# Reading the moving operand of the energy matmuls backwards in a self-attention kernel

## The chip, the cores and the metric

The kernel runs on one core of a Trainium2 chip. The metric is the device time of one execution in microseconds (us). TensorE is called PE in the profile, and its weight loads, which run beside its matmuls, are shown as an engine of their own, PEld. VectorE is DVE, ScalarE is ACT, GpSimd is POOL, SyncE is SP.

## The reference

The input x has the shape (4, 64, 64, 256): four images b, each with N = 4096 positions. Per image:

- q = x Wq + bq and k = x Wk + bk, 128 channels each; v = x Wv + bv, 256 channels.
- q, k and v are taken as matrices with N columns by reshaping the flat array, not by transposing it (`q.reshape(B, -1, N)`).
- energy[n, m] = sum over c of q[c, n] k[c, m]; attention = softmax over m; out[c, n] = sum over m of v[c, m] attention[n, m].
- The result is gamma * out + x, all in float32.

A query n is a column of q; whatever order the columns are worked on in, each has its own softmax and its own output column.

## The kernel before, in words

**Tiles and loops.** Per image b there are 16 groups g of 256 queries (NB = 256, NJ = 2 halves j of 128), and per group 8 steps t of 4 blocks of 128 keys each, 128 steps u = 8 g + t per image and 512 in all. Every float32 product is made of three float32r products: each operand is split into a high half h, a remainder l and a combined form d (`halved`, lines 260 to 269; `halves`, 352 to 361).

**One step on TensorE** is 36 matmuls, each with a weight load of its own (128 columns):

- *Energies* (`energy`, lines 317 to 339): 12 matmuls at line 330. The weights are a 128x128 block of k in form f (tile `k`), the moving operand is the whole form f of q, 256 columns (tile `q`). Two of three go to the PSUM tile `sa`, the third to `sb`. They are made three steps ahead (LOOK = 3): while step u is attended, the energies of u + 3 are made. ScalarE takes the exponential (line 334), VectorE multiplies the two parts (344), ScalarE and VectorE make h, l and d of the result (349, 355, 358).
- *Attend* (`attend`, lines 363 to 391): 24 matmuls at line 380, in the order h, l, d; within each, half j = 0 and then 1; within each half, four key blocks i = 0 to 3. The weights are 128 columns of h, l or d, the moving operand is a row of `vh`, `vl` (258 columns, two of ones for the softmax sums) or `vd` (256 columns). The row is m = 2t + i // 2 + 16 (i % 2). The h and l products of half j are added up in the PSUM tile `a`*j* over the whole group, the d products in `bb`. So the last four products of l (j = 1) stand directly before the eight of d.

Rows of `vh` and `vl` lie 260 elements apart, those of `vd` 256; the tiles of q and k have rows of 256 and 128 elements.

**Order of the work.** The order is written out by hand (`manual_schedule`). In each step of the main loop (lines 507 to 549): the energies of u + 3 in two halves k = 0, 1, `join` and `upper` after the first, then the weights of a later step are fetched by `load_k` on POOL's queue, then `halves`, then `attend`, with pieces of the finish of the previous group between (`proceed`). While a group is finished (`finish`, lines 400 to 422), VectorE scales the sums, TensorE transposes the 256 queries back (line 417, tile `ot`, once in a group), VectorE adds the input `xr` to it (line 421) and POOL's queue writes the result out (422). The very last group has its own form, `finish_last` (lines 440 to 466), with two adds at line 465 and the last write on SP's queue. Between two images, 16 rounds of projections (lines 116 to 173) run through TensorE, with the first energies beside them.

Three tiles named `pad` (lines 208 to 212) hold nothing and shift the addresses of the pools after them.

Of the kernel before, what the change touches and what calls it, by code (L numbers as in the profile page):

```python
# [13 lines left out]
ALU = mybir.AluOpType  # L14
# [6 lines left out]
def kernel(  # L21
# [36 lines left out]
    nc = tc.nc  # L58
    B, W, H, C = x.shape
    P = 128  # L60
# [115 lines left out]
    NJ = NB // P  # L176
# [24 lines left out]
    with ExitStack() as fast:  # L201
# [115 lines left out]
        def energy(b, u, k):  # L317

            g, t = divmod(u, NU)
            if k == 0:  # L320
                x = ppool.tile([P, 4, NB], F32, tag="x", name=f"x_{b}_{u}", bufs=3)
                y = ppool.tile([P, 4, NB], F32, tag="y", name=f"y_{b}_{u}")
                units[b, u] = x, y
            x, y = units[b, u]
            q, kt = loads[b, "q", g], loads[b, "k", u]
            sa = ps_s.tile([P, 2, NJ, P], F32, tag="a", name=f"sa_{b}_{u}_{k}")
            sb = ps_s.tile([P, 2, NJ, P], F32, tag="b", name=f"sb_{b}_{u}_{k}")
            for i in range(2):
                for to, f, first, last in ((sa, 0, True, False), (sa, 1, False, True), (sb, 2, True, True)):
                    nc.tensor.matmul(  # L330
                        to[:, i], kt[:, 2 * k + i, f, :], q[:, f], start=first, stop=last
                    )
            for to, sp, scale in ((x, sa, (1.0 + E) / E), (y, sb, -1.0 / E)):
                nc.scalar.activation(  # L334
                    to[:, 2 * k : 2 * k + 2, :],
                    sp.rearrange("p i j d -> p i (j d)"),
                    AF.Exp,
                    scale=scale,
                )
# [23 lines left out]
        def attend(b, u):  # L363

            g, t = divmod(u, NU)
            if t == 0:
                now["acc"] = [
                    ps_o.tile([P, C + 2], F32, tag=f"a{j}", name=f"a{j}_{b}_{g}")
                    for j in range(NJ)
                ]  # L370
                now["bb"] = ps_o.tile([P, NJ, C], F32, tag="bb", name=f"bb_{b}_{g}")
            h, l, d = units[b, u]
            acc, bb = now["acc"], now["bb"]
            for left, right in ((h, vh), (l, vl), (d, vd)):
                for j in range(NJ):
                    out_ = bb[:, j, :] if left is d else acc[j]
                    for i in range(4):
                        m = 2 * t + i // 2 + NI * (i % 2)

                        nc.tensor.matmul(  # L380
                            out_,
                            left[:, i, j * P : (j + 1) * P],
                            right[:, m, : out_.shape[1]],
                            start=(t == i == 0 and (left is h or left is d and j == 0)),
                            stop=(t == NU - 1 and i == 3 and left is not h),
                            skip_group_check=True,
                        )
            if t == NU - 1 and (b, g) != (B - 1, NG - 1):
                o = now["o"] = work.tile([P, NJ, C + 2], F32, tag="o", name=f"o_{b}_{g}")
                for j in range(NJ):  # L390
                    nc.scalar.activation(o[:, j, :], acc[j], AF.Identity, scale=1.0 + E)

        def factors(b, g, gamma):

            r = work.tile([P, 2, NJ], F32, tag="r", name=f"r_{b}_{g}")
            nc.vector.reciprocal(r[:, 0, :], zall[:, b * NG + g, :])
            nc.vector.tensor_tensor(r[:, 0, :], r[:, 0, :], gamma.to_broadcast([P, NJ]), ALU.mult)
            return r[:, 0, :], r[:, 1, :]

        def finish(b, g, o, bb, xr):  # L400
            yield
            yield

            nc.vector.tensor_copy(zall[:, b * NG + g, :], o[:, :, C])
            r, _ = factors(b, g, gam1)
            nc.vector.tensor_tensor(o[:, :, :C], o[:, :, :C], bb, ALU.add)
            yield
            for j in range(NJ):
                nc.scalar.activation(
                    o[:, j, :C], o[:, j, :C], AF.Identity, scale=r[:, j : j + 1]  # L410
                )
            yield
            yield
            tp = ps_t.tile([P, 2, NB], F32, tag="t", name=f"ot_{b}_{g}")
            for s in range(2):
                for j in range(NJ):
                    nc.tensor.transpose(
                        tp[:, s, j * P : (j + 1) * P], o[:, j, s * P : (s + 1) * P], ident
                    )
            yield  # L420
            nc.vector.tensor_tensor(xr, xr, tp, ALU.add)
            nc.gpsimd.dma_start(ov[b, g], xr)

        def guard():

            z = zall.rearrange("p n j -> p (n j)")
            ok = ppool.tile([P, 4, NB], F32, tag="y", name="ok")[:, 0, : B * NG * NJ]
            nc.vector.tensor_scalar(ok, z, Z_LOW, None, ALU.is_ge)
            nc.vector.scalar_tensor_tensor(ok, z, Z_HIGH, ok, ALU.is_le, ALU.mult)
            yield  # L430
            nc.vector.tensor_reduce(zs, ok, AX.X, ALU.min)
            nc.vector.tensor_scalar(zs, zs, 0.5, None, ALU.is_lt)
            zp = ps_s.tile([P, 1], F32, tag="b", name="zp")
            nc.tensor.matmul(zp, ones, zs, start=True, stop=True)
            yield
            nc.vector.tensor_copy(again, zp)
            yield
            yield

        def finish_last(b, g, xr):  # L440

            for j in range(NJ):
                a = now["acc"][j]
                nc.vector.tensor_copy(zall[:, b * NG + g, j : j + 1], a[:, C : C + 1])
            r, ra = factors(b, g, gam)
            check = guard()
            nc.vector.tensor_scalar(ra, r, 1.0 + E, None, ALU.mult)
            o = work.tile([P, NJ, C + 2], F32, tag="o", name=f"o_{b}_{g}")
            tps = []
            for j in range(NJ):  # L450
                next(check)
                nc.scalar.activation(
                    o[:, j, :C], now["bb"][:, j, :], AF.Identity, scale=r[:, j : j + 1]
                )
                nc.vector.scalar_tensor_tensor(
                    o[:, j, :C], now["acc"][j][:, :C], ra[:, j : j + 1], o[:, j, :C], ALU.mult, ALU.add
                )
                tp = (ps_t, ps_s)[j].tile([P, 2, P], F32, tag="ta"[j], name=f"ot_{b}_{g}_{j}")
                for s in range(2):
                    nc.tensor.transpose(tp[:, s, :], o[:, j, s * P : (s + 1) * P], ident)  # L460
                tps.append(tp)
            for j in range(NJ):
                next(check)
                n = slice(j * P, (j + 1) * P)
                nc.vector.tensor_tensor(xr[:, :, n], xr[:, :, n], tps[j], ALU.add)
            nc.sync.dma_start(ov[b, g], xr)

        def begin(b, i):

            if i == 5:  # L470
                load_q(b, 0)
            if i == 9:
                for _ in halve_q(b, 0):
                    pass
            if i in (4, 6, 8):
                load_k(b, i // 2 - 2)
            if i >= 10:
                energy(b, (i - 10) // 2, i % 2)
            if i in (12, 14):
                join(b, i // 2 - 6)  # L480
            if i in (13, 15):
                upper(b, i // 2 - 6)
                load_k(b, i // 2 - 3)

        image(0)
        for b in range(B):
# [20 lines left out]
            for u in range(STEPS):  # L507
                g, t = divmod(u, NU)
# [36 lines left out]
                if (b, u) == (B - 1, STEPS - 1):  # L545
                    finish_last(b, g, loads.pop((b, "x", g)))
                elif t == NU - 1:
                    start(finish(b, g, now["o"], now["bb"], loads.pop((b, "x", g))))
# [9 lines left out]
    NJ = NB // P  # L558
    NP = NM // 2
    xg, og = columns(x, NB), columns(out, NB)  # L560
    with tc.If(nc.values_load(again[0:1, 0:1]) > 0), ExitStack() as general:
# [8 lines left out]
        for b in range(B):  # L570
# [16 lines left out]
            for g in range(NG):  # L587
                ps = []
                mx = work.tile([P, 2, NB], F32, tag="mx", name=f"gmx_{b}_{g}")
                for t in range(NP):  # L590
                    sp = ps_s.tile([P, 2, NB], F32, tag="s", name=f"gs_{b}_{g}_{t}")
                    for h in range(2):
# [4 lines left out]
                            start=True,  # L597
                            stop=True,
                        )
                    p = ppool.tile([P, 2, NB], F32, tag="p", name=f"gp_{b}_{g}_{t}")  # L600
# [6 lines left out]
                tp = ps_t.tile([P, NJ, P], F32, tag="t", name=f"gmt_{b}_{g}")  # L607
# [22 lines left out]
                for t, p in enumerate(ps):  # L630
# [8 lines left out]
                    for h in range(2):  # L639
                        for s in range(2):  # L640
# [4 lines left out]
                                start=(t == h == 0),  # L645
                                stop=(2 * t + h == NM - 1),
                            )
                xr = xpool.tile([P, 2, NB], F32, tag="xr", name=f"gxr_{b}_{g}")
# [41 lines left out]
```

## Time and profile before

The median of three runs is 2455.51 us (2453.16 to 2455.78). One more run with the profiler took 2453.05 us; its span from the first to the last instruction is 2451.3 us.

| engine | busy us | share of the span | instructions |
|---|---|---|---|
| PE (matmuls) | 2438.7 | 99% | 19982 |
| PEld (weight loads) | 2408.0 | 98% | 19982 |
| DVE | 2099.0 | 86% | 2314 |
| ACT | 1795.2 | 73% | 3201 |
| POOL | 424.5 | 17% | 781 |

Matmuls are pipelined, and the profile's busy time of PE is the time in which at least one is under way, so its "mean ns of one" (some 280 ns) is the latency of a matmul and not its share of the time. What a matmul costs in a stream is read from the starts of successive stretches in the timeline. The mean granted TensorE clock was 0.999 of full speed.

The whole idle time of PE that the view of waits names is a few microseconds: 2.4 us at the start for the identity, 0.8 us for the first x and 1.1 us in the last group.

### The profile page before, as it was taken

The numbers are of one execution on the slowest core, as the hardware profiler recorded it, in microseconds if no ns is written. First come the engines' busy times: TensorE is split into PE (matmuls) and PEld (weight loads), VectorE is DVE, ScalarE is ACT, GpSimd is POOL, SyncE is SP. The second block draws the span as 40 slices with busy tenths as digits, with TensorE's granted clock in tenths as the row PEclk, the third lists the DMA queues.
The fourth block names the chain that finished last, engine by engine and source line by source line (L and its number), as shares of the span: only waits on it lengthen the run. The fifth ranks groups of instructions, "written<-read, shape, count | busy, mean of one in ns | idle before, by whom it ended". The sixth has DMA issues, their size and how long they took to land.

```text
span 2451.3 us, 50024 instructions
## 1 busy us (share of the span) xinstructions
PE 2438.7 (99%) x19982; PEld 2408.0 (98%) x19982; DVE 2099.0 (86%) x2314; ACT 1795.2 (73%) x3201; POOL 424.5 (17%) x781
## 2 busy tenths in 40 slices
PE   9999999999999999999999999999999999999998
PEld 8999999999899999999989999999998999999998
DVE  5988888888698888888869888888886988888887
ACT  5777777776677777777667777777766777777775
POOL 4211111111411111111141111111114111111110
PEclk9999999999999999999999999999999999999999
DMA  7766666665776666666477666666647766666663
GB/s 234 224 202 209 204 207 202 202 215 153 235 221 197 210 203 208 208 197 213 141 243 226 203 203 202 208 210 201 206 140 248 223 204 201 204 207 210 203 202 111
DMA packets 137407, 498.92 MB, mean 204 GB/s; under 512 B 15536, under 2 KB 57264, under 8 KB 137168
## 3 DMA queue, kind: packets, MB, share of 16 engines
q0 software_dynamic: 92320, 453.17, 60.0%
q1 hardware_dynamic: 44304, 42.22, 5.5%
q8 instruction: 160, 2.62, 0.4%
q14 instruction: 79, 0.65, 0.1%
q10 hardware_dynamic: 544, 0.26, 0.0%
HBM read 445.25 MB, written 50.33 MB: 202 GB/s over the span
## 4 chain that ended last, share of the span: by engine, by line


## 5 line engine op out<-in xcount | busy, mean ns | idle before, releaser
L334 ACT ACTIVATE x<-sa 128x512 f32<-128x512 f32 x1024 | 612.2, 598 | 516.1 <-PE sa L330 514.0
L344 DVE TENSOR_TENSOR x<-x,y 128x1024 f32<-128x1024 f32 x512 | 626.2, 1223 | 234.4 <-ACT y L334 234.4
L330 PE MATMUL sa<-q,k 128*128 128x256 f32 x4096 | 735.4, 279 | 0.0
L358 DVE SCALAR_TENSOR_TENSOR d<-h,x 128x1024 fp32r<-128x1024 f32 x512 | 623.3, 1217 | 0.0
L355 DVE TENSOR_TENSOR l<-x,h 128x1024 fp32r<-128x1024 f32 x512 | 623.2, 1217 | 0.0
L330 PEld LDWEIGHTS sa<-q,k 128*128 128x128 f32 x4096 | 619.4, 188 | 0.4
L334 ACT ACTIVATE y<-sb 128x512 f32<-128x512 f32 x1024 | 615.7, 601 | 0.0
L380 PE MATMUL a<-vh,h 128*128 128x258 f32 x4096 | 574.4, 283 | 0.0
L380 PE MATMUL a<-vl,l 128*128 128x258 f32 x4096 | 572.8, 282 | 0.0
L330 PE MATMUL sb<-q,k 128*128 128x256 f32 x2048 | 567.1, 277 | 0.0
L380 PE MATMUL bb<-vd,d 128*128 128x256 f32 x4096 | 558.6, 279 | 0.0
L314 POOL DMA_DIRECT2D k<-kf x512 | 279.1, 545 | 1573.3 <-PE sb L330 1548.3
L349 ACT ACTIVATE h<-x 128x1024 fp32r<-128x1024 f32 x512 | 543.8, 1062 | 8.3 <-DVE x L344 7.8
L380 PEld LDWEIGHTS a<-vl,l 128*128 128x128 f32 x4096 | 525.3, 189 | 0.0
L380 PEld LDWEIGHTS a<-vh,h 128*128 128x128 f32 x4096 | 522.9, 189 | 0.0
L380 PEld LDWEIGHTS bb<-vd,d 128*128 128x128 f32 x4096 | 515.1, 188 | 0.0
L330 PEld LDWEIGHTS sb<-q,k 128*128 128x128 f32 x2048 | 384.5, 188 | 0.1
L137 PE MATMUL qk<-wqk_sb,xts 128*128 128x256 f32 x512 | 121.0, 379 | 0.0
L158 PE MATMUL v<-xts,wv_sb 128*128 128x256 f32 x512 | 120.3, 379 | 0.0
L158 PEld LDWEIGHTS v<-xts,wv_sb 128*128 128x128 f32 x512 | 97.3, 190 | 13.2
L137 PEld LDWEIGHTS qk<-wqk_sb,xts 128*128 128x128 f32 x512 | 92.3, 190 | 10.0
L275 POOL DMA_DIRECT2D qd<-qks x128 | 69.2, 549 | 179.8 <-DVE qks L146 170.6
(56 smaller groups left out, 864.4 us busy)
## 6 DMA issues: line engine op xcount, KB each, us to landing
k<-kf POOLq DMA_DIRECT2D x512, 768.0 KB, 4.7
x<-in_x_dram SPq DMA_DIRECT2D x128, 256.0 KB, 3.9
kf<-f POOLq DMA_DIRECT2D x64, 384.0 KB, 4.0
out_dram<-x POOLq DMA_DIRECT2D x63, 256.0 KB, 2.5
qd<-qks POOLq DMA_DIRECT2D x128, 64.0 KB, 3.0
qr<-qd SPq DMA_DIRECT2D x64, 128.0 KB, 3.6
wv_sb<-in_L_conv_Wv_dram POOLq DMA_DIRECT2D x1, 256.0 KB, 5.7
out_dram<-x SPq DMA_DIRECT2D x1, 256.0 KB, 3.8
```

The lines of the kernel that those rows point to most:

```text
L137: nc.tensor.matmul(qk[:, s, :], self.xt[i][:, k, s, :], wqk_sb[:, k, :], start=(k == 0), stop=(k == KC - 1),)
L158: nc.tensor.matmul(vp[:, eh, :], wv_sb[:, k, eh * P : (eh + 1) * P], self.xt[i][:, k].rearrange("p s a -> p (s a)"), start=(k == 0), stop= ...
L275: nc.gpsimd.dma_start(qd[b, i // 2 + NG // 2 * s][:, i % 2, :], x[:, s, :C2])
L314: nc.gpsimd.dma_start(t.rearrange("p (i s) f d -> p i s (f d)", s=2), kf[b, u % NU])
L330: nc.tensor.matmul(to[:, i], kt[:, 2 * k + i, f, :], q[:, f], start=first, stop=last)
L334: nc.scalar.activation(to[:, 2 * k : 2 * k + 2, :], sp.rearrange("p i j d -> p i (j d)"), AF.Exp, scale=scale,)
L344: nc.vector.tensor_tensor(x, x, y, ALU.mult)
L349: nc.scalar.activation(h, units[b, u], AF.Identity, scale=UPPER)
L355: nc.vector.tensor_tensor(l, x, h.bitcast(F32), ALU.subtract)
L358: nc.vector.scalar_tensor_tensor(d, h.bitcast(F32), 1.0 + E, x, ALU.mult, ALU.subtract)
L380: nc.tensor.matmul(out_, left[:, i, j * P : (j + 1) * P], right[:, m, : out_.shape[1]], start=(t == i == 0 and (left is h or left is d and ...
```

## The change

- At line 330 the moving operand q is flattened to 256 columns and read with a step of -1, from the last column to the first. The energies of a group then have their queries in reverse order, and so have h, l and d, the halves j of the sums, and the transposed result.
- At line 421 (and 465 for the last group, where half j now holds the other half of the queries) the add reads and writes `xr` with a step of -1, so that each query meets its own input; the result is written out as before.
- In `attend`, in steps t = 1 and t = 3 alone, the four products of l for j = 1 run through i = 3, 2, 1, 0. Neither of these steps holds the first or the last product of a sum.

```
 for to, f, first, last in ((sa, 0, True, False), (sa, 1, False, True), (sb, 2, True, True)):
     nc.tensor.matmul(
-        to[:, i], kt[:, 2 * k + i, f, :], q[:, f], start=first, stop=last
+        to[:, i],
+        kt[:, 2 * k + i, f, :],
+        q[:, f].rearrange("p j d -> p (j d)")[:, ::-1],
+        start=first,
+        stop=last,
     )
...
 for left, right in ((h, vh), (l, vl), (d, vd)):
     for j in range(NJ):
         out_ = bb[:, j, :] if left is d else acc[j]
-        for i in range(4):
+        back = left is l and j == NJ - 1 and t in (1, 3)
+        for i in reversed(range(4)) if back else range(4):
             m = 2 * t + i // 2 + NI * (i % 2)
...
 yield
-nc.vector.tensor_tensor(xr, xr, tp, ALU.add)
+x = xr[:, :, ::-1]
+nc.vector.tensor_tensor(x, x, tp, ALU.add)
 nc.gpsimd.dma_start(ov[b, g], xr)
...
 for j in range(NJ):
     next(check)
-    n = slice(j * P, (j + 1) * P)
-    nc.vector.tensor_tensor(xr[:, :, n], xr[:, :, n], tps[j], ALU.add)
+    x = xr[:, :, (1 - j) * P : (2 - j) * P][:, :, ::-1]
+    nc.vector.tensor_tensor(x, x, tps[j], ALU.add)
 nc.sync.dma_start(ov[b, g], xr)
```

## The prediction, made before the changed kernel ran

> **What bounds the kernel now.** I read the page's engine table and costliest groups first. All 36 matmuls of a step belong to lines 330 and 380, and none of their groups has idle time before it:
>
> ```profile
> PE 2438.7 (99%) x19982; PEld 2408.0 (98%) x19982; DVE 2099.0 (86%) x2314; ACT 1795.2 (73%) x3201; POOL 424.5 (17%) x781
> ...
> L330 PE MATMUL sa<-q,k 128*128 128x256 f32 x4096 | 735.4, 279 | 0.0
> ...
> L380 PE MATMUL a<-vl,l 128*128 128x258 f32 x4096 | 572.8, 282 | 0.0
> L330 PE MATMUL sb<-q,k 128*128 128x256 f32 x2048 | 567.1, 277 | 0.0
> L380 PE MATMUL bb<-vd,d 128*128 128x256 f32 x4096 | 558.6, 279 | 0.0
> ```
>
> The reader sees a kernel that TensorE alone limits: no wait is left to remove, and only the pace of the matmul stream can move the end. The page has no chain of waits to show here. So I went to the timeline of PE, and took the pace as the distance between the starts of neighbouring stretches divided by the matmuls between them. This is from step t = 3 of a group in the middle of the run to the first matmul of t = 5:
>
> ```profile
> 1003.82 1.12 PE L380 MATMUL a<-vl,l 128*128 128x258 f32 x8
> 1004.78 1.11 PE L380 MATMUL bb<-vd,d 128*128 128x256 f32 x8
> 1005.73 0.40 PE L330 MATMUL sa<-q,k 128*128 128x256 f32 x2
> ...
> 1007.14 1.12 PE L380 MATMUL a<-vh,h 128*128 128x258 f32 x8
> 1008.10 1.12 PE L380 MATMUL a<-vl,l 128*128 128x258 f32 x8
> 1009.05 1.09 PE L380 MATMUL bb<-vd,d 128*128 128x256 f32 x8
> 1009.99 0.39 PE L330 MATMUL sa<-q,k 128*128 128x256 f32 x2
> 1010.21 0.28 PE L330 MATMUL sb<-q,k 128*128 128x256 f32 x1
> ...
> 1011.35 0.28 PE L380 MATMUL a<-vh,h 128*128 128x258 f32 x1
> ```
>
> The same twelve energies take 1.41 us (1005.73 to 1007.14, 117.5 ns each) after t = 3 and 1.36 us (1009.99 to 1011.35, 113.3 ns each) after t = 4. Nothing in the program differs between them but the step before. The eight d products before the wide twelve take 0.95 us; elsewhere in this group they take 0.92 to 0.94. The h and l products take 0.95 to 0.96 us for eight, 119 ns each, though their operand is only two columns longer. In a group of another image (412 to 449 us) the same place is wide again: 1.42 us after t = 3, 1.36 us in its other steps, so this belongs to the position and is no disturbance. It looks like two phases of one stream, call them tight and wide, of which the wide one is carried on until something breaks it: after t = 1 the d products are wide as well (0.94 us), but there the transposes at line 417 come between, and the energies behind them run at 113 ns again.
>
> The timeline of the weight loads shows what the tight phase rests on. For the `sb` product that starts at 1010.21 in the fence above:
>
> ```profile
> 1010.10 0.19 PEld L330 LDWEIGHTS sb<-q,k 128*128 128x128 f32 x1
> ```
>
> Its load starts 0.11 us ahead, together with the matmul before it. Loads and matmuls therefore run in pairs, and about 110 of the 113.3 ns lie between a load's start and its own matmul. I take 113.3 ns as a floor that the weight loads set and that a different reading order of q can't lower, since the loads are not changed.
>
> **What the Trainium skill says.** "TensorE: Matmul & The Clock Gate", section "LDWEIGHTS (loading the stationary operand)", prices a load at columns / 1.2, which is 106.7 ns for 128. The trace's 110 ns from load to matmul agrees with a small surcharge. The same page, "Step-by-step: what each phase is for", gives the moving operand and the loads a read port each and says that one takes no bandwidth from the other. The two paces above don't prove it wrong, but something lets identical instructions differ by 4.2 ns; that these two reads disturb each other is my inference, since no other engine's work shows at those places. "SBUF — State Buffer", section "Door 1: The DMA port swizzle", says that successive accesses within one 16-byte line run at full rate. A step of -1 still makes four accesses to each line, so it is no reason for half the rate; no row before has a backward moving read. "Vector Engine (DVE) Microarchitecture Reference", section "5.1 Performance modes — why throughput varies by op and dtype", lists an operand with a negative step as not measured.
>
> **The change part by part.** The sum is made against the profiled span of 2451.3 us; that run took 2453.05 us and the median of the others is 2455.51, so I apply the difference to 2455.5.
>
> 1. *Energies read backwards.* Same 6144 matmuls, same loads, same columns. 768 of them (12 in each of 64 groups) are wide now. If backward reading keeps the floor and the wide phase isn't carried through, each such stretch goes from 1.41 to 1.36 us: 64 x 0.05 = 3.2 us less. It lies wholly on the path. Bounds: the best would be the pace of the fp32 transposes of 128 columns in the same trace (four in 0.43 us from load to load, about 108 ns): 6144 x 5 = 31 us less; the worst, all energies in the wide phase, is 4.2 ns x 5376 = 23 us more. I take -3.2.
> 2. *Four l products reversed at t = 1 and 3.* These are exactly the steps whose d products run wide. Nothing is added: four operands change places, v is resident, the l tile comes from one instruction, so no wait moves. If the other order of addresses puts the stream into the tight phase before d, the eight d products fall from 0.95 and 0.94 to the 0.92 us seen after t = 6 or t = 0: 0.03 + 0.02, times 64, 3.2 us less. Bounds: nothing gained, or the eight l products of the same step change too by 0.01 to 0.02 us either way, 128 x 0.02 = 2.6 us. I take -3.2.
> 3. *New phase at the entry of the h products.* Unknown in sign; h stretches vary between 0.95 and 0.98 us from step to step. With 0.01 us over 512 steps the bound is 5 us either way; I take 0.
> 4. *The adds at lines 421 and 465.* 63 adds of 679 ns. If a backward step doubled them, DVE would have 0.7 us more in a group of 34.1 us (t = 3 at 1002.87 to the next at 1037.00), in which it is 88% busy (stretch 500 to 600 us) and so idle for 4 us. I cost it at nothing: PE's stream hides it. Behind the add, POOL's queue holds the write (line 422) and then the loads of k, which are issued nearly two steps, some 7 us, before use and land in 4.7 us, so 0.7 us fits. Only the two adds of the last group (0.75 us together) are on the end's path: 0 to 0.8 us more. I take 0.
>
> Sum: -3.2 - 3.2 = -6.4 us, which gives 2449.1; I say **2449 us** (-0.26%).
>
> **The rivals.**
>
> - *Nothing measurable.* The reordered l products end in the wide phase again and the energies carry it on as now. For it: the h and l products hardly repeat their pace from step to step, so a single new order may land anywhere. Against: 7 of 8 steps do arrive at the energies in the tight phase or are reset. Time: 2455.
> - *Faster by more.* The 113.3 ns contains a disturbance that backward reading removes. For it: the transposes' 108 ns, with the same weight columns. Against: 113.3 ns is the same for every pair of q and k addresses and for the d products, as a fixed cost would be. Half the bound: 6144 x 2.5 + 6.4 = 22 us less, 2434.
> - *Slower: backward reading itself holds the energies in the wide phase.* The place is line 330 and the price 4.2 ns a matmul. Now one energy in eight is wide, and part 2 may give 3.2 us, so it decides from the point where wide energies x 4.2 ns exceed 3.2 + 3.2 us, about 1,520 of 6144, a quarter. For it: the reads' relative direction changes for every energy, and a pattern that suits two of three products says nothing of another. Against: nothing measured. With all wide and no gain at d: 2455 + 23 = 2478; with half wide, 2462.
> - *A backward fp32r read at half the rate* would add some 107 ns x 6144 (the energies' column time, estimated from the skill's 2.4 GHz on the TensorE page), over 650 us. Four hits in a line speak against it; 2 in 100, outside the range.
>
> **How the numbers follow.** Forecast 46% (38 faster, 8 within 0.2%), since part 1 and part 2 can each fail; its own range is 2443 to 2453. Nothing measurable 13% (11 within, 1 either side). Faster by more 18%. Slower 23% (22 slower, 1 within), the half rate included. 0.2% is 4.9 us, about what a measurement of this kernel can tell from no change. Faster 0.57, same 0.20, slower 0.23. The range reaches from 2426, near the end that part 1's best bound makes, to 2478, all energies wide.
>
> **What would show it.** In the timeline of the changed kernel: the energies after t = 3 at 1.36 us for twelve, the d stretches of t = 1 and t = 3 at 0.92 to 0.93 us, the other energies still at 113.3 ns, h and l near 0.95 us, line 421 near 679 ns, and no new wait for PE. Energies below 1.36 us break the floor of the loads; energies at 1.41 us in most steps are the slower rival; h and l stretches that move by more than 0.01 us mean that part 3 was the larger term.

## The result, and the profile after

The changed kernel takes 2472.06 us (median of 4 runs, 2470.34 to 2472.65), against 2454.34 us for the kernel before beside it (4 runs). The ratio is 1.0071 with a 95% interval of [1.0053, 1.0088]: it is slower, by 17.7 us. Its profiled span is 2470.3 us, 19.0 us longer than the one before, at the same granted clock (0.998 and 0.999).

The page of the changed kernel, engine table and groups of line 331 (330 before) and of the d products:

```profile
PE 2458.3 (100%) x19982; PEld 2426.9 (98%) x19982; DVE 2099.6 (85%) x2314; ACT 1797.1 (73%) x3201; POOL 425.0 (17%) x781
...
L331 PE MATMUL sa<-q,k 128*128 128x256 f32 x4096 | 755.4, 282 | 0.0
...
L331 PE MATMUL sb<-q,k 128*128 128x256 f32 x2048 | 577.5, 282 | 0.0
...
L388 PE MATMUL bb<-vd,d 128*128 128x256 f32 x4096 | 552.5, 277 | 0.0
```

TensorE is busy 19.6 us longer and waits for nothing new; DVE, ACT and POOL are busy within 2 us of before. The energies are busier (735.4 to 755.4 and 567.1 to 577.5 us), the d products less (558.6 to 552.5 us). The timeline of PE shows how. Step t = 3 of a group of the changed kernel:

```profile
1012.78 1.12 PE L388 MATMUL a<-vl,l 128*128 128x258 f32 x8
1013.73 1.08 PE L388 MATMUL bb<-vd,d 128*128 128x256 f32 x8
1014.65 0.40 PE L331 MATMUL sa<-q,k 128*128 128x256 f32 x2
...
1016.07 0.40 PE L388 MATMUL a<-vh,h 128*128 128x258 f32 x2
```

The d products take 0.92 us (1013.73 to 1014.65) where they took 0.95, so they are tight now; but the twelve energies behind them take 1.42 us (1014.65 to 1016.07) all the same, 118 ns each. Before the change, tight d products were followed by energies of 1.36 us.

For the whole run I took the distance from each matmul's start to the next one's from the trace. "Above 113.3" sums what exceeds 113.33 ns (340 ns for three) over all matmuls of a kind, gaps of over 135 ns (with a wait or with other work in them) left out; the means are those of the main loop, without the energies between two images:

| matmuls | before: mean ns, by t | above 113.3, us | after: mean ns, by t | above 113.3, us |
|---|---|---|---|---|
| energies (6144) | 113.3 to 114.0; 117.8 in one t of 8 | 4.7 | 117.7 to 117.8 in all | 26.6 |
| h (4096) | 118.9 to 121.5 | 26.6 | 118.6 to 122.5 | 27.1 |
| l (4096) | 118.1 to 120.4 | 25.2 | 118.1 to 120.8 | 26.0 |
| d (4096) | 114.5 to 116.3; 118.0 and 118.5 at t = 1 and 3 | 11.1 | 113.4 to 115.1 | 5.0 |

With every gap counted, the energies are 21.6 us longer, the d products 6.2 shorter, h and l 1.4 longer, the projections of q and k 1.7 and the transposes 0.5 longer: 19.0 us, the whole difference of the spans. The 1.7 us can't be put down to the change: those projections take 110.6 us in the trace of the kernel before and 112.2 in that of the changed one, but 110.6 again in `e6_k_shift256` below, which reads q backwards too. What is left is two effects of opposite sign, both in the pace of TensorE's stream.

The starts also show that "wide" is not one state. The wide energies after t = 3 of the kernel before come at 117.5, 118.3, 117.5 ns over and over, the backward ones of the changed kernel at 115.0, 118.3, 120.0. Three of either take 353.3 ns, so the mean is the same, 117.8.

### The profile page after: what moved, and what is told of

The parts are those of the page before. It is cut to its first block, busy times and chain, and to the rows that moved or that the text cites. A ratio compares the mean times of both kernels' runs of the same rounds, so it can differ in the third digit from the quotient of the medians.

```text
span 2470.3 us, 50092 instructions
## 1 busy us (share of the span) xinstructions
PE 2458.3 (100%) x19982; PEld 2426.9 (98%) x19982; DVE 2099.6 (85%) x2314; ACT 1797.1 (73%) x3201; POOL 425.0 (17%) x781
## 4 chain that ended last, share of the span: by engine, by line
## 5 line engine op out<-in xcount | busy, mean ns | idle before, releaser
L331 PE MATMUL sa<-q,k 128*128 128x256 f32 x4096 | 755.4, 282 | 0.0
L331 PE MATMUL sb<-q,k 128*128 128x256 f32 x2048 | 577.5, 282 | 0.0
L388 PE MATMUL bb<-vd,d 128*128 128x256 f32 x4096 | 552.5, 277 | 0.0
L388 PEld LDWEIGHTS bb<-vd,d 128*128 128x128 f32 x4096 | 509.9, 188 | 0.0
```

Of the source, the lines that this page charges most:

```text
L331: nc.tensor.matmul(to[:, i], kt[:, 2 * k + i, f, :], q[:, f].rearrange("p j d -> p (j d)")[:, ::-1], start=first, stop=last,)
L388: nc.tensor.matmul(out_, left[:, i, j * P : (j + 1) * P], right[:, m, : out_.shape[1]], start=(t == i == 0 and (left is h or left is d and ...
```

## The experiments

"Wide" and "tight" are the prediction's words: near 117.7 ns and 113.3 ns for a product of 256 columns. Paces come from the starts, as in the table above.

**Each part alone.** `e1_q_only` is the changed kernel without the reversed l products, `e2_back_only` the kernel before with them and nothing else.

```
-for i in reversed(range(4)) if back else range(4):     # e1_q_only: from the changed kernel
+for i in range(4):
...
-for i in range(4):                                     # e2_back_only: from the kernel before
+back = left is l and j == NJ - 1 and t in (1, 3)
+for i in reversed(range(4)) if back else range(4):
```

> The changed kernel with the l products in their old order; q is still read backwards. Theory: the backward reading alone puts all energies at 117.8 ns and costs 4.4 ns x 5376 = 24 us, and the reversed l products win about 3 us back at the d products of t = 1 and 3: 2475 us, with d wide there. Rival: the backward energies hand the h products another phase, and this alone makes d tight: 2472 us, d at 113.3 ns in t = 1 and 3.

> The kernel before with the four l products reversed at t = 1 and 3 and nothing else. Theory: d tight at t = 1 and 3 and the energies after t = 3 tight with it: 64 x (0.05 + 0.05) = 6.4 us less, 2448 us. Rival: the order helps only behind backward energies, and here nothing moves: 2454 us.

`e1_q_only`: 2477.94 us against 2455.56 (ratio 1.0091, [1.0076, 1.0107]). All energies at 117.7 to 117.9 ns; d is wide at t = 3 (118.5) but not at t = 1 (115.5), 8.5 us above 113.3. So the backward energies alone cost 22.4 us, and both readings of the d products hold in part: in the changed kernel t = 1 is mended mostly by the backward energies (118.0 to 115.5 ns, and 114.6 with the order of l), t = 3 by the order of l (118.5 to 114.9).

`e2_back_only`: 2450.30 us against 2455.56 (13 and 17 runs, ratio 0.9978, [0.9969, 0.9986]). Step t = 3 in its timeline:

```profile
1038.40 1.12 PE L381 MATMUL a<-vl,l 128*128 128x258 f32 x8
1039.35 1.08 PE L381 MATMUL bb<-vd,d 128*128 128x256 f32 x8
1040.27 0.39 PE L330 MATMUL sa<-q,k 128*128 128x256 f32 x2
...
1041.63 0.52 PE L381 MATMUL a<-vh,h 128*128 128x258 f32 x3
```

d takes 0.92 us and the energies 1.36 (1040.27 to 1041.63): the wide phase is no longer made at t = 3, and so not carried on. At t = 1 the same reordering does little: d goes from 118.0 to 117.1 ns. And a new loss appears behind the transposes that follow t = 1: there 28 of 60 groups now have wide energies, none before, which takes back 1.1 of the 3.4 us won at the energies after t = 3. This half of the change still beats both kernels.

**Backward in another operand.** `e3_d_backward` reads vd backwards and q forwards.

```
-right[:, m, : out_.shape[1]],
+right[:, m, ::-1] if left is d else right[:, m, : out_.shape[1]],
```

> The kernel before with the d products' moving operand vd read from its last column to its first (the d part then lies in reverse channel order in the output). Theory: a backward moving read holds the wide phase whatever the operand: the d products end at 117.8 ns in all steps, about 4.4 ns x 3100 = 14 us more, and the energies after them start wide, up to 20 us more again. Rival: the loss belongs to q's and k's addresses alone, and d stays at 113.3 ns in the steps where it is there now: 2454 us.

2468.4 us in one run beside 2455.56. d goes to 117.6 to 120.5 ns in every step (23.5 us above 113.3, in place of 11.1). Its timeline, at a step where d was tight before:

```profile
1008.02 1.11 PE L380 MATMUL bb<-vd,d 128*128 128x256 f32 x8
1008.96 0.41 PE L330 MATMUL sa<-q,k 128*128 128x256 f32 x2
...
1010.34 1.11 PE L380 MATMUL a<-vh,h 128*128 128x258 f32 x8
```

The energies behind take 1.38 us (1008.96 to 1010.34): by the starts the first one to three are above 114 ns and the rest at 113 to 114. In this run the wide phase of the backward reads isn't carried on by the forward reads after them, against the second half of the expectation.

**Which part of "backwards" costs.** q is cut into pieces of e columns; the pieces run from last to first, or only the columns within a piece do. The cut shows the pieces of 4 columns; `e5_within_lines` has the step of -1 on the last axis in place of the middle one.

```
-kt[:, 2 * k + i, f, :], q[:, f], start=first, stop=last
+kt[:, 2 * k + i, f, :], q[:, f].rearrange("p j d -> p (j d)").rearrange("p (c e) -> p c e", e=4)[:, ::-1, :], start=first, stop=last
```

> The kernel before with q read in pieces of 4 columns (16 bytes), the pieces from last to first and the columns within each forwards (queries of a group come out permuted). Theory (what matters is which way the moving read walks through the memory): 117.8 ns as in the changed kernel, about 2475 us. Rival (the step of -1 within a 16-byte piece is what costs): 113.3 ns, about 2454 us.

> The kernel before with q read in pieces of 4 columns (16 bytes), the pieces forwards and the columns within each from last to first (queries of a group come out permuted). The walk of the moving read through the memory is what costs, the step of -1 is not: 113.3 ns, about 2454 us. Rival: some of the 4.4 ns belongs to the step of -1, 114 to 118 ns, up to 2477 us.

> The kernel before with q read in pieces of 16 columns (64 bytes), the pieces from last to first and forwards within each. If the walk counts 16 bytes at a time, three of four steps are forwards now and the energies come back to 113.3 ns, 2454 us; if it counts in rows of 64 bytes or more, they stay at 117.8 ns, 2477 us.

> The kernel before with q read in pieces of 32 columns (128 bytes), the pieces from last to first and forwards within each. Each jump leads to a place 256 bytes before the one where a forward walk would go on. With a period of 256 bytes: 113.3 ns, 2454 us. With one of 512: near 118 ns, about 2480 us.

> The kernel before with the two halves of q exchanged, each read forwards (pieces of 128 columns, 512 bytes). A fully forward walk but for one jump: 113.3 ns, 2454 us. Rival: what counts is where the read of one matmul ends and that of the next begins (here the end of one half and the start of the other, no longer the end and the start of the row): near 117.8 ns.

| run | pieces, bytes | order | energies, ns | time, us (before beside it) |
|---|---|---|---|---|
| `e5_within_lines` | 16 | backwards within only | 113.3 to 113.9 | 2453.99 (2456.31) |
| `e4_lines_backward` | 16 | pieces backwards | 117.7 to 117.9 | 2477.72 (2455.56) |
| `e11_pieces16` | 64 | pieces backwards | 117.7 to 118.2 | 2481.92 (2456.31) |
| `e11_pieces32` | 128 | pieces backwards | 115.9 to 118.0 | 2478.35 (2454.08) |
| `e11_pieces128` | 512 | halves exchanged | 113.3 to 114.0 | 2454.12 (2456.31) |

(The one wide t of the kernel before, 117.8 ns, is left out of the first and last row; it is there as before.) The step of -1 costs nothing. The order of pieces costs all of it, up to pieces of 128 bytes, while exchanging halves of 512 bytes leaves every step as it was.

**Is it the weight read?** The prediction took it that the moving read and the weight read disturb each other. Two runs read the weights at a step of 0, so that their read has no walk; one moves the k tiles.

```
-kt[:, 2 * k + i, f, :],
+kt[:, 2 * k + i, f, :1].to_broadcast([P, P]),      # e8 from the changed kernel, e9 from the kernel before
...
-pool("pad3", 1).tile([P, 48], F32, name="pad3")
+pool("pad3", 1).tile([P, 112], F32, name="pad3")   # e6
```

> The changed kernel with the energies' weights read at a step of 0, so that each load takes one key's column 128 times (every energy is that of the first key of its block). Theory (the moving read and the weight read disturb each other, and which way they walk past each other decides): a load that stays at one place has no walk, so the direction of q no longer matters, and this run and its forward twin have the same pace at line 331, near 113.3 ns: about 2450 us. Rival (a backward moving read costs by itself): the energies stay at 117.8 ns, 2472 us.

> The kernel before with the energies' weights read at a step of 0, as in the run beside it. Theory: the same pace as that run, near 113.3 ns, about 2454 us. Rival: 113.3 ns here and 117.8 ns there, 20 us apart.

> The changed kernel with the k tiles 256 bytes further on in each partition (pad3 is 64 columns longer). Theory (the opposite walk costs in itself, not where it begins): energies at 117.8 ns again, 2472 us. Rival (the addresses of q and k happen to suit the forward walk only): another place brings the energies to 113.3 ns, about 2448 us.

Twelve energies in the timeline of e8, and then of e9:

```profile
1013.46 0.40 PE L331 MATMUL sa<-q,k 128*128 128x256 f32 x2
...
1014.88 0.40 PE L388 MATMUL a<-vh,h 128*128 128x258 f32 x2
```

```profile
1003.05 0.39 PE L330 MATMUL sa<-q,k 128*128 128x256 f32 x2
...
1004.41 0.40 PE L380 MATMUL a<-vh,h 128*128 128x258 f32 x2
```

1.42 us backwards, 1.36 us forwards; 2477.20 and 2453.12 us. In the means 117.6 to 118.1 ns and 113.3 to 115.0. With k 256 bytes on, every mean of the changed kernel's table comes back to a tenth (2471.27 us). As an account of the backward loss, the theory of two reads that walk past each other has fallen: the loss stays when the weight read has no walk or lies elsewhere. The weight read isn't without effect, though. In e9 the d products of t = 3 are wide as before (118.6 ns), but the energies behind them come at 117.5, 113.3, 119.2 and 116.7 ns and then at 113.3, 114.4 in the mean, where the kernel before holds 117.8 for all twelve. Why is open.

**Is 113.3 ns a floor of the weight loads?** `e12_fewer_columns` reads d backwards and gives both d and l 240 columns.

```
+w = 240 if left is l or left is d and (t, i) != (0, 0) else out_.shape[1]
...
-out_,
+out_[:, :w],
...
-right[:, m, : out_.shape[1]],
+right[:, m, w - 1 :: -1] if left is d else right[:, m, :w],
```

> The kernel before with d's moving operand read backwards as in e3 and with 240 columns in place of 256 (but for the first product of each sum), and with 240 columns in place of 258 in all l products, forwards (16 channels of l's and d's part and l's share of the sums are left out). Theory (113.3 ns is the floor of the weight loads, and what lies above it is the moving stream): 16 columns fewer are 6.7 ns, so backward d goes from 117.8 to 120 ns down to 113.3, l from 119.6 to 113.3, and neither falls below it: 2468 - 23 - 25 = 2420 us. Rival (the extra time is a fixed cost of a matmul, whatever its columns): d at 118 to 120 ns and l near 119 ns as before, about 2466 us. Third: both below 113.3 ns, if the floor isn't the loads'.

```profile
1000.57 1.12 PE L381 MATMUL a<-vh,h 128*128 128x258 f32 x8
1001.53 1.06 PE L381 MATMUL a<-vl,l 128*128 128x240 f32 x8
1002.43 1.06 PE L381 MATMUL bb<-vd,d 128*128 128x240 f32 x8
1003.33 0.40 PE L330 MATMUL sa<-q,k 128*128 128x256 f32 x2
...
1004.71 1.14 PE L381 MATMUL a<-vh,h 128*128 128x258 f32 x8
```

Eight l products take 0.90 us (1001.53 to 1002.43), 112.5 ns each, where the eight h products ahead, with 258 columns and their loads unchanged, take 0.96. Over the run l lies at 111.9 to 112.7 ns and d at 111.9 to 113.4, and one gap in eight of these is at 109 ns or less, where neither the kernel before nor the changed one has any. So the third reading holds: 113.3 ns is no floor of the loads. The 18 columns fewer took 7.1 ns from l in the mean, close to the 7.5 ns that 18 columns take at the N / 2.4 of the Trainium skill ("TensorE: Matmul & The Clock Gate", section "Back-to-back issue gap"), and 16 fewer took 6.6 ns from backward d (119.1 in e3 to 112.4). So the pace of these products follows the number of moving columns. With N / 2.4 taken off, an estimate by that page, h, l and backward d carry some 12 ns more per matmul on average, the backward energies 11, and tight rows of 256 columns 6.7. All of it is more than the 2.5 ns that the section has for isolated matmuls, and the measurement decides. No run gave tight energies fewer columns.

The time was 2422.54 us, near the 2420 of the theory that failed, and that is luck: l and d lost more than it allowed, and the energies, whose reads weren't touched, lost their tight phase. They run at 114.7 to 118.2 ns here, 10.3 us more over the run; the twelve in the fence take 1.38 us (1003.33 to 1004.71).

**Where the next read begins.** If forward rows are special, breaking them up should lose the 113.3 ns without any backward read. `e13` and `e16` set the rows of q 260 and 272 columns apart (16 and 64 bytes off), `e15` exchanges halves in one of the three forms, `e17` reads backwards with rows 264 columns apart (32 bytes off) and has the l products in their old order.

```
-t = work.tile([P, 3, NJ, P], F32R, tag="q", name=f"q_{b}_{g}")
+t = work.tile([P, 3, NB + 4], F32R, tag="q", name=f"q_{b}_{g}")     # e13; e16: NB + 16; e17: NB + 8
+t = t[:, :, :NB].rearrange("p f (j d) -> p f j d", d=P)
...
-kt[:, 2 * k + i, f, :], q[:, f], start=first, stop=last              # e15
+kt[:, 2 * k + i, f, :], q[:, f].rearrange("p j d -> p (j d)").rearrange("p (c e) -> p c e", e=P)[:, :: -1 if f == 1 else 1, :], start=first, stop=last
```

> The kernel before with the three rows of q 260 columns apart in place of 256, so that each matmul's read begins 16 bytes further on, within 1024, than the one before ended. Theory (the seam counts: a read must go on, within 1024 bytes, where the last one ended): the energies leave 113.3 ns for 117 to 120 ns, 20 to 40 us more. Rival (only the walk within a matmul counts): 113.3 ns, 2454 us.

> The kernel before with the two halves of q exchanged in the matmuls of form f = 1 alone, each half forwards (the energies' high parts come out permuted against each other). Seam theory with a period of 1024 bytes: two of three seams jump by 512 bytes and the energies go to 117 ns or more, 2475 us. Seam theory with a period of 512 or less, or no seam at all: 113.3 ns, 2454 us.

> The kernel before with the three rows of q 272 columns apart, so that each matmul's read begins 64 bytes further on than the one before ended; forwards. Seam theory with a period of 64 bytes: 113.3 ns, 2454 us. With a period of 128 to 512 bytes: near 117.7 ns as with 16 bytes, 2479 us.

> The kernel before with q read backwards and its three rows 264 columns apart: a read that ends at the first 16 bytes of a row is followed by one that begins 16 bytes above that place, within 64 bytes, in two of three cases, as it would be forwards. If the loss of the backward read is a seam alone: two of three energies return to 113.3 ns, about 115 ns in the mean and 2462 us. If it is the backward walk: 117.7 ns, about 2478 us.

Twelve forward energies of e13:

```profile
1013.58 0.40 PE L331 MATMUL sa<-q,k 128*128 128x256 f32 x2
...
1015.00 0.40 PE L381 MATMUL a<-vh,h 128*128 128x258 f32 x2
```

1.42 us, as in the changed kernel, with every read forwards. Means and times: e13 117.7 to 118.2 ns, 2479.35 us; e16 116.4 to 117.3 ns, 2476.38 us; e15 the table of the kernel before, 2457.26 us; e17 117.9 to 118.3 ns, 2483.53 us. So starts that are 16 or 64 bytes off lose the tight phase as a backward read does, and starts that are 512 bytes off don't. The 512 rest on e15: with all three forms exchanged, as in `e11_pieces128`, each read again begins where the last one ended, counted within 1024 bytes. Two things weren't tested apart: whether the distance from the last read counts or the place of the start itself, and what the wider q tile does by moving the tiles behind it (for k, e6 tried 256 bytes alone). e17 says that a backward walk isn't mended by placing its starts that way.

**Can h and l be mended so?** `e10_rows_in_turn` takes h's and l's blocks in the order 0, 2, 1, 3; `e14_v_in_order` stores all v rows in the order of their use.

```
-for i in range(4):                                        # e10
+for i in range(4) if left is d else (0, 2, 1, 3):
...
-m = slice(2 * i, 2 * i + 2)                               # e14, in halve_v
+r = 4 * (i % (NI // 2)) + i // (NI // 2)
+m = slice(r, r + 3, 2)
...
-m = 2 * t + i // 2 + NI * (i % 2)                         # e14, in attend
+m = 4 * t + i
```

> The kernel before with the four key blocks of h and l in the order i = 0, 2, 1, 3, so that neighbouring rows of vh and vl (16 bytes apart within 1024) follow each other, where now every matmul moves on by about 256. Theory (the two reads settle in the tight phase when their distance stays the same from matmul to matmul): the h and l products fall from 119.6 ns towards 116, up to 3.5 x 8192 = 29 us less, 2426 us. Rival (258 columns cost that much wherever they lie): 119.6 ns, 2454 us within 5 us.

> The kernel before with the rows of vh, vl and vd stored in the order in which the steps read them (row 4 t + i in place of 2 t + i // 2 + 16 (i % 2)), so that three of four reads of h and l go on where the last one ended. Seam theory: h and l fall from 119.6 ns towards 258 columns + 6.7 ns, 114.2 ns, for most of 8192 products: 20 to 40 us less, 2415 to 2435 us. Rival (only the walk counts, or 258 columns cost 12 ns wherever they lie): 119.6 ns, 2454 us within 5 us.

Neither: 2459.06 us in one run beside 2456.11, and 2473.01 against 2455.89 us (ratio 1.0072, [1.0055, 1.0089]). h and l stay at 118.3 to 121.3 ns. In e14, d is wide at every even t (117.7 ns) and so are the energies behind each of them (117.7 to 117.8): a loss at d that the forward reads behind carry on, as at t = 3 of the kernel before. At odd t the first d products are wide and the last ones tight, and the energies behind are tight at t = 3, 5 and 7. At t = 1 the transposes come between:

```profile
1005.11 1.10 PE L381 MATMUL bb<-vd,d 128*128 128x256 f32 x8
1006.05 0.60 PE L418 MATMUL ot<-ident,o 128*128 128x128 f32 x4
1006.40 0.48 PE L331 MATMUL sa<-q,k 128*128 128x256 f32 x2
1006.72 0.28 PE L331 MATMUL sb<-q,k 128*128 128x256 f32 x1
...
1007.90 1.12 PE L381 MATMUL a<-vh,h 128*128 128x258 f32 x8
```

The last ten energies take 1.18 us (1006.72 to 1007.90), 118 ns each: wide, behind d products that ended tight. So it is in 28 of the 60 groups of e14 with transposes there, as in e2. In the kernel before, the energies after t = 1 are tight in all 60 groups with transposes and wide in the four without, the first of each image. That speaks for transposes ending a wide phase there; in e2 and e14 they can start one.

A row of 258 columns, 1032 bytes, doesn't run tight in either order; whether its two extra columns or its distance of 1040 bytes is to blame wasn't separated.

## Why the prediction went wrong, step by step

- **Step 1, energies read backwards, failed.** It was costed at -3.2 us on the ground that backward reading keeps the floor, so that the tight phase is what the energies settle into and only the step at t = 3 upsets it. The trace shows +21.6 us. Tight is not where any read of 256 columns comes to rest: backward, shifted and reversed piecewise reads never stayed there, and forward reads of unshifted rows mostly did, unless wide products, transposes or, in e12, shortened ones stood before them. Seven tight steps of eight were read as a property of the matmul, where they were one of the addresses, and every energy before had the same.
- **The premise under it, that 113.3 ns is a floor of the weight loads, failed too**: e12 has l and d products at 112.4 ns in the mean, one in eight at 109 ns or less, with the same loads. The load that starts with the matmul before it showed how the two are paired, not which of them sets the pace.
- **The inference that the two reads disturb each other failed** as the ground of the backward loss: 117.6 to 118.1 ns with weights at a step of 0 (e8), 117.7 to 117.8 with k moved (e6). The Trainium skill's statement that each has its own port ("TensorE: Matmul & The Clock Gate", "Step-by-step: what each phase is for") agrees with that much; the shortened wide stretch of e9 leaves open whether it is all.
- **Step 2, the reversed l products, held in its mechanism at t = 3 and hardly at t = 1.** Predicted -3.2 us at d and, with part 1's stretch behind t = 3, -6.4 in all. Alone it gave -5.3 us: by the starts d -2.3 (-1.9 at t = 3, -0.5 at t = 1), l -0.8, energies -2.2. In the changed kernel it gave -5.9 us (2477.94 to 2472.06), of which 1.2 came at the d products of t = 4, which the prediction doesn't have.
- **Step 3, the entry of h and l**, was bounded at 5 us and is +1.4. **Step 4, the adds**, was costed at nothing, and the changed kernel's groups agree, 679 ns before and 680 after:

```profile
L430 DVE TENSOR_TENSOR x<-x,ot 128x512 f32<-128x512 f32 x63 | 42.8, 680 | 0.0
```

- **The rival that came true** is "backward reading itself holds the energies in the wide phase". Its price, 4.2 ns x 5376 = 23 us, was right to 1.4 us, partly by luck: the backward energies aren't held in the wide phase of t = 3, but run in an order of their own that has the same mean. Its time of 2478 assumed no gain at d, and 6.2 us came back there. It was given 23% on the ground that nothing measured spoke for it. Nothing measured spoke for the forecast either: no backward moving read stood in the trace.

## What to carry to other kernels

Where TensorE's stream is the bound, take the pace from the starts of the matmuls, step by step, before and after: an average over a group hides that identical instructions run at 113 and at 118 ns. A pace that is the same at every place in a trace may still be earned by the layout; test it with one shifted or shortened operand before calling it a floor. And run the parts of a change apart: here one part was worth 5 us and the other cost 22.

## What the runs showed of the hardware

- fp32r products of 256 moving columns with a weight load each ran at 113.3 ns in most steps when the moving reads went forwards and each began, modulo 512 bytes, where the last one ended; exchanging 512-byte halves kept that. Starts 16 or 64 bytes off, pieces of 16 to 128 bytes in reverse, and a fully backward read gave 116 to 118 ns.
- Such forward reads also ran at 117.8 ns for all twelve matmuls behind a wide stretch (t = 3 of the kernel before, the even steps of e14), or lost it within three (e3) or four (e9). Transposes between ended it in the kernel before, and were followed by wide energies in 28 of 60 groups of e2 and e14.
- A step of -1 within 16 bytes and weights moved by 256 bytes didn't change the pace. Weights at a step of 0 left forward energies at 113.3 ns in six steps of eight and backward ones at 117.6 to 118.1, but the wide stretch after t = 3 ended early (e9).
- Eighteen columns fewer took 7.1 ns from an l product and 16 fewer took 6.6 ns from a backward d product, down to 112.4 ns in the mean with the same weight loads (e12).
- A VectorE add of 128x512 float32 with one PSUM input took 680 ns with a step of -1 on its SBUF operands, 679 without.
- What in the memory or in TensorE has the 512 bytes, whether the start or its distance from the last read counts, and why rows of 258 columns never settled at a tight pace, is open.
